# A mixture of experts behind an attention: the experts' rows in fixed slots of 512, what is left over by table

## The chip, the cores and the metric

The kernel runs on one core of a Trainium2 chip. Its five engines run side by side, each with its own queue of instructions that it works off in order: TensorE (PE in the profile, with its weight loads as PEld), VectorE (DVE), ScalarE (ACT), GpSimd (POOL) and SyncE (SP, which here only issues transfers). The metric is the device time of one execution in microseconds. Before the change it is 1090.66 us, the median of three runs (1090.1 to 1093.66).

## The reference

The input x is 4 batches of 1024 rows of 256. The first half is causal attention with 16 heads, whose projections go through a latent space, followed by a residual and a layer norm. The second half is a mixture of 8 experts with a Sinkhorn router:

```
scores = (x @ router_w.T + router_b) / temp
gates  = sinkhorn(scores)                     # 3 rounds over experts and over the rows of a batch
topk_vals, topk_idx = top_k(gates, 2)
topk_gates = topk_vals / sum(topk_vals)
expert e: (relu(x @ wg[e]) * (x @ wp[e])) @ wo[e]      # 256 -> 512 -> 256
x = layernorm(x + sum of the two picked experts, weighted by topk_gates)
```

Each row is wanted by two of the eight experts, so there are 8192 pairs of a row and an expert. The kernel computes only these pairs, not all 8 experts for each row. How many pairs an expert gets depends on the data.

## The kernel before

**The stages.** The attention runs batch by batch; the projections of the next batch and the output projection and routing of the one before are woven into it. Routing needs a whole batch, since Sinkhorn normalises over its rows. The pairs of batches 0 to 2 are therefore known during the attention of batch 3, and those of batch 3 only after it. The expert stage begins when the attention ends, with slots whose rows belong to the first three batches, while the last half batch is finished and routed beside them. At the end all rows are read back, normalised and written out.

**Lists and slots.** `pairs` is a table in device memory with a region for each expert. `route` works out for each pair its place in its expert's region and writes it there with indirect transfers on POOL (L808), 16 for each batch. `lay_out` turns the experts' counts into a table of slots, of 256 rows each: which expert, and where its rows begin. It is made twice: `lay_out(0)` for 17 slots that are surely full after three batches, `lay_out(1)` for the rest, up to 39 in all. SP reads expert and place from the table into registers (`value`, L896). 35 slots run always (`SURE`); if the data needs more, a branch runs the others (L1183).

**One slot.** `pairs_of` loads the list of 256 rows (L920), `weights` the expert's three weight matrices, 512 KB each (L943), `gather` the rows with two indirect transfers on POOL (L929). `rows` transposes the rows on TensorE (L973). All matrices are split into a high and a low part of fewer bits (`split`: ACT casts, L188, and DVE subtracts, L189), and a product is three matmuls (`mm3`, L195 to L197). `halves` does this for the weights, in 6 pieces of 512 columns. `slot` then makes, for each of four chunks f of the hidden size, the gate and the linear part in one PSUM bank of 512 columns, 256 for each (tile gp, from a ring of three banks); ACT takes the relu (L995), DVE multiplies (L996), and the result is split. After that come two output tiles (eo), which ACT scales (L1009) and POOL adds onto `results` in device memory with an indirect transfer (L1010). The adds of a slot wait for the landing of those of the slot before, since they may touch the same rows.

**Order.** `begin` is a generator: while slot n runs, it issues the transfers of later slots (`fetch`: lists 4 ahead, weights 2, gathers 3), transposes the rows of slot n + 1 and splits its weights. Weight tiles have two buffers as loaded and two as split, gathered rows three, eo six. A scheduler decides the final order of the instructions on each engine from priorities and its own estimate; on the engines that order is fixed. `in_turn` and `apart` only tell it which accesses may or may not pass one another.

Of the kernel before, what the change touches and what calls it, by code (L numbers as in the profile page):

```python
# [9 lines left out]
F32 = mybir.dt.float32  # L10
# [8 lines left out]
W_BUFS, GA, EA, EO = (2,3,4,6)  # L19
# [3 lines left out]
XG = 3  # L23
SCAT3 = 0.4
SH_A, SH_B, NSA = ((),(),0)
DZ = 3
SURE = 35
# [8 lines left out]
P = 128  # L36
# [7 lines left out]
def kernel(  # L44
# [35 lines left out]
    BT = B * T  # L80
    SR = 256
    RB = SR // P

    NA = -(-(2 * (B - 1) * T - E * (SR - 1)) // SR)
    NSLOT = (2 * BT + E * (SR - 1)) // SR
    REGION = BT + SR
    NLIST = (E - 1) * REGION + NSLOT * SR
# [12 lines left out]
    attn = actx.enter_context(tc.tile_pool(name="attn", bufs=1, side="right"))  # L100
    pctx = ctx.enter_context(ExitStack())
# [296 lines left out]
    def attend(unit):  # L398
# [25 lines left out]
        for g, qc in [(g, qc) for g in gs for qc in qcs]:  # L424
            q, k = stack(unit, g)
            for kb in range((qc + 1) * BPQ):
                lo = max(0, kb * P - qc * QC)
                n = f"{b}_{g}_{qc}_{kb}"
                pT = work.tile([P, HG, QC], F32, tag="pT", name=f"pT{n}", bufs=PT_BUFS)
# [33 lines left out]
    results = dram.tile([BT + SR, C], F32, name="results")  # L463
# [3 lines left out]
    base = const.tile([P, E], F32, name="base")  # L467
    for e in range(E):
        nc.gpsimd.memset(rank[:, e : e + 1], float(E - e))
        nc.gpsimd.memset(base[:, e : e + 1], float(e * REGION))  # L470
    ones = const.tile([P, P], F32, name="ones")
# [9 lines left out]
    slot_i = const.tile([1, NSLOT], I32, name="slot_i")  # L481
    nc.gpsimd.iota(slot_i, pattern=[[1, NSLOT]], base=0, channel_multiplier=0)
    slot_no = const.tile([1, NSLOT], F32, name="slot_no")
    nc.gpsimd.tensor_copy(slot_no, slot_i)

    def prepare():
# [5 lines left out]
        no_pair = work.tile([P, HG * QC], F32, tag="pT", name="no_pair", bufs=PT_BUFS)  # L492
        no_pair = no_pair[:, : 4 * PER].bitcast(I32).rearrange("p (n w) -> p n w", w=4)
        nc.gpsimd.iota(no_pair[:, :, 3], pattern=[[1, PER]], base=0, channel_multiplier=PER)
        nc.vector.tensor_single_scalar(no_pair[:, :, 0], no_pair[:, :, 3], SR - 1, ALU.bitwise_and)
# [5 lines left out]
            in_=mask[:, :C].unsqueeze(1).to_broadcast([P, RB, C]),  # L501
# [149 lines left out]
    def route(b):  # L651
# [141 lines left out]
        nc.vector.tensor_tensor(base, base, ps[:, NE : NE + E], ALU.add)  # L793
        at = sinkp.tile([P, 2, NB], F32, tag="so_a", name=f"so_a{b}")
# [26 lines left out]
    shift = tab("shift", [2, E])  # L821
    for e in range(E):
        nc.gpsimd.memset(shift[:, 0, e : e + 1], float(e * REGION))
        nc.gpsimd.memset(shift[:, 1, e : e + 1], float(e * REGION - SR + 1))
    zero = tab("zero", [E])
    nc.gpsimd.memset(zero, 0.0)
    used = zero
    tables = {}

    def lay_out(which):  # L830

        nonlocal used
        n_slots = NSLOT - NA if which else NA

        def t_(name, shape=(E,)):
            return tab(f"{name}{which}", shape)

        need = t_("need")
        nc.vector.tensor_tensor(need, base[:1], shift[:, which], ALU.subtract)
        needi = small.tile([1, E], I32, tag=f"needi{which}", name=f"needi{which}", bufs=1)  # L840
# [3 lines left out]
        nc.vector.tensor_tensor(need, need, used, ALU.subtract)  # L844
        yield 0.0
        upto = need
        for n in (1, 2, 4):
            nxt = t_(f"upto{n}")
            nc.vector.tensor_copy(nxt[:, :n], upto[:, :n])
            nc.vector.tensor_tensor(nxt[:, n:], upto[:, n:], upto[:, : E - n], ALU.add)  # L850
            upto = nxt
            yield 0.0
        hop = t_("hop")
        nc.vector.tensor_scalar(hop, need, -float(SR), float(REGION), ALU.mult, ALU.add)
        if which:
            more = t_("more")
            nc.vector.tensor_tensor(more[:, : E - 1], used[:, 1:], used[:, : E - 1], ALU.subtract)
            nc.vector.scalar_tensor_tensor(
                hop[:, : E - 1], more[:, : E - 1], float(SR), hop[:, : E - 1], ALU.mult, ALU.add
            )  # L860
        yield 0.0
        no = slot_no[:, :n_slots]
        past = t_("past", (n_slots, E - 1))
        nc.vector.tensor_tensor(
            past, no.unsqueeze(2).to_broadcast([1, n_slots, E - 1]),
            upto[:, : E - 1].unsqueeze(1).to_broadcast([1, n_slots, E - 1]), ALU.is_ge,
        )
        yield 0.0
        table = t_("table", (2, n_slots))
        nc.vector.tensor_reduce(table[:, 0], past, AX.X, ALU.add)  # L870
        nc.vector.tensor_tensor(
            past, past, hop[:, : E - 1].unsqueeze(1).to_broadcast([1, n_slots, E - 1]), ALU.mult
# [3 lines left out]
        nc.vector.scalar_tensor_tensor(table[:, 1], no, float(SR), table[:, 1], ALU.mult, ALU.add)  # L876
        if which:
            first = t_("first", (1,))
            nc.vector.tensor_scalar(first, used[:, :1], float(SR), None, ALU.mult)
            nc.vector.tensor_scalar(table[:, 1], table[:, 1], first, None, ALU.add)  # L880
        tablei = tables[which] = small.tile([1, 2, n_slots], I32, tag=f"ti{which}", name=f"ti{which}", bufs=1)
        nc.vector.tensor_copy(tablei, table)
        if which:
            tables["filled"] = small.tile([1, 1], I32, name="filled", bufs=1)
            nc.vector.tensor_copy(tables["filled"], upto[:, E - 1 :])
        if not which:

            used = t_("used")
            nc.vector.tensor_tensor(used, upto, need, ALU.subtract)
            nc.vector.tensor_scalar(used, used, -1.0, float(NA), ALU.mult, ALU.add)  # L890
            nc.vector.tensor_scalar_max(used, used, 0.0)
            nc.vector.tensor_tensor(used, used, need, ALU.min)
# [3 lines left out]
    def value(which, r, s, top):  # L896
        return nc.values_load(
            tables[which][0:1, r, s : s + 1], engines=[mybir.EngineType.SP], min_val=0, max_val=top,
            skip_runtime_bounds_check_because="worked out on the chip from counts that add up to 2 * B * T",
        )  # L900
# [10 lines left out]
    slots = {}  # L911

    def name_of(key):
        return f"{key[0]}_{key[1]}"

    def pairs_of(key):
        which, s = key
        row = value(which, 1, s, NLIST - SR)
        ent = const.tile([P, RB, 4], I32, name=f"ent_{name_of(key)}")
        ins = nc.sync.dma_start(out=ent, in_=pairs[bass.ds(row, SR)].rearrange("(p j) w -> p j w", j=RB))  # L920
        if not which:
            apart("pairs", "early", ins, ("last",))
        slots[key] = [ent, None, None, [], []]

    def gather(key):
        which = key[0]
        xg = slots[key][1] = early.tile([P, RB, C], F32, tag="xg", name=f"xg{name_of(key)}", bufs=XG)
        for j in range(RB):
            ins = nc.gpsimd.indirect_dma_start(  # L929
                out=xg[:, j], out_offset=None, in_=x1_rows[: BT if which else BT - T],  # L930
                in_offset=bass.IndirectOffsetOnAxis(ap=slots[key][0][:, j, 0:1], axis=0),
            )
            if not which:
                in_turn(ins)
                apart("x1", "early", ins, ("last",))

    def weights(key):
        which, s = key
        e = value(which, 0, s, E - 1)
        ws = slots[key][2] = []  # L940
        for i, (w, k, f) in enumerate(((wg_in, CC, FF), (wp_in, CC, FF), (wo_in, NFC, C))):
# [373 lines left out]
```

## Time and profile before

| | |
|---|---|
| time, median of three runs | 1090.66 us |
| the profiled execution, its own time | 1088.8 us |
| its span | 1087.1 us |
| busy TensorE / VectorE / ScalarE / GpSimd | 974.8 / 821.6 / 707.8 / 492.4 us |
| granted clock of TensorE over the span | 0.968 |
| moved by DMA | 146.33 MB |

The page gives busy time by engine, and the windows give the same for a stretch of the span. A busy TensorE is not TensorE at its peak: matmuls overlap, and the profile models their ends, so the distance from one start to the next tells the price of one. In a timeline a row has start, length, engine, line, operation and tiles; what stands in brackets is the idle time before it and what ended it. "SPq" is SP's queue of transfers.

### The profile page before, as it was taken

What the parts mean: (1) busy time and instruction counts of PE and PEld (TensorE: products, weight loads), DVE (VectorE), ACT (ScalarE), POOL (GpSimd) and SP (SyncE); (2) the same over time, 40 slices, a digit from 0 to 9 for tenths busy, and PEclk for the clock granted to TensorE, in tenths of its full rate; (3) what the DMA queues carried; (4) which work ended last, traced back from release to release, by engine and by line L of the source; (5) the groups of instructions that cost most, each with busy time, mean ns of one, the idle gap of its engine ahead of it and who ended that gap; (6) DMA issues with size and microseconds to landing.
All of it is one profiled execution on the core that took longest, in us unless ns stands there. A gap on an engine that the chain in (4) does not pass through costs nothing.

```text
span 1087.1 us, 20881 instructions
## 1 busy us (share of the span) xinstructions
PE 974.8 (90%) x6808; PEld 616.2 (57%) x6808; DVE 821.6 (76%) x2551; ACT 707.8 (65%) x1701; POOL 492.4 (45%) x552
## 2 busy tenths in 40 slices
PE   6689999999989999999899999999999699999940
PEld 4444333355434345533344333499999699999940
DVE  4768778888897888887538997398897588888716
ACT  3446666666776665676566776777776577877723
POOL 7167511121443624440423414645557756666545
PEclk9889999999999999999999999999999899999975
DMA  7663411231331312421123220587873788899638
GB/s 258 178 210 112 118 49 35 79 96 44 106 90 48 109 46 74 142 54 50 50 84 121 47 64 2 179 252 214 227 222 101 230 235 237 230 237 255 148 42 309
DMA packets 92065, 146.33 MB, mean 135 GB/s; under 512 B 19760, under 2 KB 55088, under 8 KB 91568
## 3 DMA queue, kind: packets, MB, share of 16 engines
q1 hardware_dynamic: 69296, 108.50, 31.6%
q0 software_dynamic: 20608, 36.18, 14.3%
q8 instruction: 56, 0.92, 0.3%
q10 hardware_dynamic: 2048, 0.27, 0.2%
q14 instruction: 57, 0.47, 0.1%
HBM read 109.26 MB, written 35.38 MB: 133 GB/s over the span
## 4 chain that ended last, share of the span: by engine, by line
PE 68%; DVE 8%; DMA 7%; ACT 6%; issue 4%; POOL 4%; SPq 2%; ACTq 0%; DVEq 0%; POOLq 0%
PE y L417 13%; PE s L354 10%; PE sT L433 9%; PE gp L195 5%; PE gp L196 5%; PE gp L197 5%; ACT pT L437 4%; POOL pairs L808 3%; PE eo L195 3%; PE eo L196 3%; PE eo L197 3%; PE po L591 2%; DVE mx L360 2%; DMA results<-eo,ent 2%; SPq L336 2%
## 5 line engine op out<-in xcount | busy, mean ns | idle before, releaser
L437 ACT ACTIVATE pT<-sT 128x512 f32<-128x512 f32 (+3 forms) x768 | 346.9, 491 | 178.4 <-PE sT L433 151.0
L363 DVE CUSTOM_DVE_ANT_0 d<-s,mask 128x128 bf16<-128x128 f32 (+3 forms) x512 | 237.0, 482 | 51.4 <-PE s L354 50.2
L433 PE MATMUL sT<-qs,ks 98*128 98x512 bf16 (+3 forms) x768 | 231.7, 328 | 16.4 <-ACT pT L437 11.6
L354 PE MATMUL s<-ks,qs 96*128 96x512 bf16 (+3 forms) x768 | 221.9, 331 | 22.5 <-DVE mx L363 7.8
L446 POOL TENSOR_SCALAR_AFFINE_SELECT pT<-pT 128x512 f32<-128x512 f32 x120 | 76.4, 637 | 273.1 <-ACT pT L437 256.8
L360 DVE TENSOR_REDUCE mx<-s 128x1 f32<-128x512 f32 x256 | 175.1, 684 | 29.4 <-PE s L354 28.3
L417 PE MATMUL y<-pT,va 128*32 128x512 f32 (+3 forms) x1536 | 181.9, 500 | 2.0 <-POOL pT L446 0.9
L1010 POOL DMA_INDIRECT results<-eo,ent x70 | 116.9, 1670 | 107.3 <-ACT hh L188 22.1
L189 DVE TENSOR_TENSOR wl<-w,wh 128x512 fp32r<-128x512 f32 x210 | 134.9, 685 | 37.7 <-ACT wh L188 37.4
L195 PE MATMUL gp<-xh,wh 128*128 128x256 f32 x560 | 159.5, 286 | 1.3 <-ACT xh L188 0.7
L197 PE MATMUL gp<-xh,wl 128*128 128x256 f32 x560 | 158.6, 284 | 0.5 <-DVE wl L189 0.5
L196 PE MATMUL gp<-xl,wh 128*128 128x256 f32 x560 | 158.9, 284 | 0.0
L354 PEld LDWEIGHTS <-qs 96*128 96x128 bf16 x768 | 71.6, 99 | 132.8 <-issue 101.0
L433 PEld LDWEIGHTS <-ks 98*128 98x128 bf16 x768 | 71.8, 98 | 122.9 <-issue 91.2
L188 ACT CAST wh<-w 128x512 fp32r<-128x512 f32 x210 | 117.6, 621 | 12.7 <-DMA w<-in_wg_dram 10.9
L195 PEld LDWEIGHTS gp<-xh,wh 128*128 128x128 f32 x560 | 106.0, 190 | 2.4 <-ACT xh L188 1.2
L197 PEld LDWEIGHTS gp<-xh,wl 128*128 128x128 f32 x560 | 106.3, 190 | 0.8 <-DVE wl L189 0.7
L196 PEld LDWEIGHTS gp<-xl,wh 128*128 128x128 f32 x560 | 106.3, 190 | 0.0
L929 POOL DMA_INDIRECT xg<-x_rows,ent x70 | 79.6, 1137 | 37.1 <-issue 17.4
L195 PE MATMUL eo<-wh,hh 128*128 128x256 f32 x280 | 80.1, 286 | 10.4 <-ACT hh L188 9.0
L808 POOL DMA_INDIRECT pairs<-ent,so_i x64 | 66.5, 1039 | 29.6 <-issue 18.4
L196 PE MATMUL eo<-wl,hh 128*128 128x256 f32 x280 | 79.1, 283 | 0.0
(207 smaller groups left out, 1603.1 us busy)
## 6 DMA issues: line engine op xcount, KB each, us to landing
w<-in_wg_dram SPq DMA_DIRECT2D x35, 512.0 KB, 6.2
w<-in_wp_dram SPq DMA_DIRECT2D x35, 512.0 KB, 5.6
w<-in_wo_dram SPq DMA_DIRECT2D x35, 512.0 KB, 4.7
ks<-parts SPq DMA_DIRECT2D x90, 128.0 KB, 2.8
qs<-parts SPq DMA_DIRECT2D x66, 128.0 KB, 2.9
parts<-lv POOLq DMA_DIRECT2D x12, 384.0 KB, 3.1
parts<-lv POOLq DMA_DIRECT2D x24, 192.0 KB, 3.1
xh<-in_x_t_dram SPq DMA_DIRECT2D x8, 512.0 KB, 5.8
```

The lines of the kernel that those rows point to most:

```text
L188: nc.scalar.copy(hi, src)
L189: (sub or nc.vector).tensor_tensor(lo, src, hi.bitcast(F32), ALU.subtract)
L195: nc.tensor.matmul(ps, lhsT=sh, rhs=mh, start=(i == 0), stop=False)
L196: nc.tensor.matmul(ps, lhsT=sh, rhs=ml, start=False, stop=False)
L197: nc.tensor.matmul(ps, lhsT=sl, rhs=mh, start=False, stop=(i == n - 1))
L354: nc.tensor.matmul(ps[:, :w], lhsT=q(h, half)[:NROW, t * P : (t + 1) * P], rhs=k(h, k0 // QC)[:NROW, :w], start=True, stop=True,)
L360: nc.vector.tensor_reduce(m, ps, AX.X, ALU.max)
L363: nc.vector.tensor_tensor_reduce(out=dump[:, :w], in0=ps[:, :w], in1=mask[:, QC - w :], scale=1.0, scalar=MASKED, op0=ALU.add, op1=ALU.max ...
L417: nc.tensor.matmul(acc[g, qc][SLOT * h : SLOT * (h + 1), lo:], lhsT=va[b % 2][:, kb, at : at + SLOT], rhs=pT[:, h, lo:], start=(kb == 0), ...
L433: nc.tensor.matmul(st[:, lo:], lhsT=k(h, kb // BPQ)[: NROW + 2, kb % BPQ * P : (kb % BPQ + 1) * P], rhs=q(h, qc)[: NROW + 2, lo:], start=T ...
L437: nc.scalar.activation(pT[:, h, lo:], st[:, lo:], AF.Exp, scale=scale)
L1010: ins = nc.gpsimd.indirect_dma_start(out=results[:, :], out_offset=bass.IndirectOffsetOnAxis(ap=ent[:, j, 1:2], axis=0), in_=eo, in_offset ...
```

## The change

The experts are no longer worked off by a table of slots of 256 rows. First come the rows 0 to 511 of each expert's region, experts 0 to 7, then the rows 512 to 1023, experts 7 to 0, and then what lies beyond row 1023, in slots of 256 rows by table. Of these three run always (`SURE = 3`), and up to 25 can be needed (`NOVER`). Expert and place of the first sixteen slots are known when the program is built, so they take no register, and the lists of all eight experts are loaded in one transfer for the first and one for the second 512. The expert that ends the first round begins the second, and its split weights are used again (`like`): so weights are split 15 times for the first sixteen slots and 3 times for the rest.

In slots of 512 rows gate and linear part have a PSUM bank each (tiles gp and lp), and the matmuls for them have 512 columns. hh and hl are now a tile for each chunk, six of each. Raw weights have one buffer instead of two, and each is loaded once the piece before it has been split; the gathered rows have two buffers of 512 rows instead of three of 256. After the third batch the counts are raised to at least 512 for each expert (`floor`), so that the last batch's pairs never fall into the first 512 rows, which are read early. `lay_out` is made once, for the rest alone. The tiles of the attention's exponentials move to a pool of their own (`exps`).

The core of the diff:

```
-W_BUFS, GA, EA, EO = (2,3,4,6)
+EO = 6
-XG = 3
+XG = 2
+HB = 6
-SURE = 35
+SURE = 3
...
+    ER = 512
     SR = 256
...
     REGION = BT + SR
-    NLIST = (E - 1) * REGION + NSLOT * SR
+    NOVER = (2 * BT - 4 * ER + 2 * (SR - 1)) // SR
+    NLIST = (E - 1) * REGION + 2 * ER + NOVER * SR
...
         nc.vector.tensor_tensor(base, base, ps[:, NE : NE + E], ALU.add)
+        if b == B - 2:
+            nc.vector.tensor_tensor(base, base, floor, ALU.max)
...
+    def pairs_of(k):
+        if k.which == 2:
+            row = value(1, k.s, NLIST - SR)
...
+        if k.which not in lists:
+            ent = lists[k.which] = const.tile([P, E, k.blocks, 4], I32, name=f"ents{k.which}")
+            regions = pairs[: E * REGION].rearrange("(e r) w -> e r w", r=REGION)
+            ins = nc.sync.dma_start(
+                out=ent.rearrange("p e j w -> p e (j w)"),
+                in_=regions[:, k.which * ER : (k.which + 1) * ER].rearrange("e (p j) w -> p e (j w)", p=P),
+            )
...
+    def weights(k, i):
+
+        if k.like is not None:
+            return
...
+        t = k.raw[i] = early.tile([P, n, f], F32, tag=f"w{i}", name=f"w{i}_{k.name}")
+        nc.sync.dma_start(out=t, in_=w[rows_e].rearrange("e (k p) f -> p (e k) f", p=P))
+
+    def halves(k, i):
+        if k.like is not None:
+            k.hl[i] = k.like.hl[i]
+            return
...
+            if 2 * R > QC:
+                gate, lin = (mx_tile(f"{i}p{k.name}_{f}") for i in "gl")
+            else:
+                both = mx_tile(f"gp{k.name}_{f}")
+                gate, lin = both[:, :R], both[:, R:]
+            for (h_, l_), ps in zip(k.hl, (gate, lin)):
+                mm3(ps, [(h_[:, c, cut], l_[:, c, cut], k.xh[:, c, :R], k.xl[:, c, :R]) for c in range(CC)])
+            r = early.tile([P, ER], F32, tag="relu", name=f"relu{k.name}_{f}", bufs=3)[:, :R]
+            nc.scalar.activation(r, gate, AF.Relu)
+            nc.vector.tensor_tensor(r, r, lin, ALU.mult)
...
+    first = [Slot(0, e) for e in range(E)]
+    second = [Slot(1, e) for e in reversed(range(E))]
+    second[0].like = first[-1]
+    further = [Slot(2, n) for n in range(NOVER)]
+
+    def begin_early():
+        pairs_of(first[0])
+        for i in range(3):
+            weights(first[0], i)
+        gather(first[0])
...
+    def begin(keys, n, given):
...
+        k, nxt = keys[n], keys[n + 1] if n + 1 < len(keys) else None
+        early_next = nxt is not None and (nxt.which == 0 or k.which > 0)
+        if n not in given and (k.which and (n == 0 or not keys[n - 1].which)):
+            pairs_of(k)
+            gather(k)
+        if early_next:
+            pairs_of(nxt)
+            gather(nxt)
...
+        for i in range(3):
+            halves(k, i)
+            if nxt is not None:
+                weights(nxt, i)
+            yield
...
+    run(first + second + further[:SURE], (0,))
...
+    with tc.If(filled > SURE):
+        added.clear()
+        with early_pool() as early, ffn_pool() as ffn:
+            run(further[SURE:])
```

## The prediction

> **What bounds the kernel now.** I read the page's busy shares first, then the windows by stage, then the timelines of the two places where TensorE stops.
>
> From part 1 of the page (engine, busy time, share of the span, instructions):
>
> ```profile
> PE 974.8 (90%) x6808; PEld 616.2 (57%) x6808; DVE 821.6 (76%) x2551; ACT 707.8 (65%) x1701; POOL 492.4 (45%) x552
> ```
>
> From the windows (stretch, then busy us and count of PE, PEld, DVE, ACT, POOL, then granted clock, DMA share, GB/s):
>
> ```profile
> 900.00:1000.00 100.00, 100.00 (x849) 100.00 (x848) 80.83 (x167) 79.83 (x191) 63.75 (x46) 1.00 0.88 236
> ...
> 1040.00:1087.00 47.00, 4.40 (x31) 3.63 (x29) 17.90 (x78) 11.77 (x24) 22.95 (x38) 0.58 0.62 196
> ```
> ```profile
> 840.00:850.00 10.00, 3.68 (x32) 3.47 (x30) 0.42 (x1) 0.39 (x1) 7.87 (x8) 0.81 0.33 73
> 850.00:860.00 10.00, 7.66 (x49) 7.66 (x50) 7.29 (x15) 7.71 (x17) 7.87 (x8) 0.68 1.03 321
> ```
>
> The attention ends and the expert stage begins at about 703.7 us; its last matmul ends near 1045.1. In that stage TensorE is never free except in one hole around 843 to 852, so the stage lasts as long as its matmuls. ACT and DVE are at 80% beside it and hidden. After 1045 TensorE is done and something else sets the end.
>
> How long a matmul takes is read from starts, because ends are modelled. Timeline of PE, first with 512 columns (the projection), then with 256 (an expert slot); start, modelled duration, engine, line:
>
> ```profile
> 17.54 0.40 PE L195 MATMUL qk_ps<-xT_h,wqk_h 128*128 128x512 f32 x1
> ...
> 19.81 0.39 PE L196 MATMUL qk_ps<-xT_l,wqk_h 128*128 128x512 f32 x1
> ```
> ```profile
> 912.27 0.28 PE L195 MATMUL gp<-xh,wh 128*128 128x256 f32 x1
> ...
> 914.05 0.28 PE L195 MATMUL eo<-wh,hh 128*128 128x256 f32 x1
> ```
>
> Ten steps in 2.27 us are 227 ns with 512 columns (230 over all undisturbed neighbours in the projection); fifteen in 1.78 are 118.7 ns with 256 (118.5 over all). That is nearly the same price per column, so the narrow matmul isn't far from streaming already.
>
> The hole, in SP's queue and on ACT:
>
> ```profile
> 826.25 0.37 SPq L943 DMA_DIRECT2D w<-in_wo_dram  x1
> 845.54 0.35 SPq L920 DMA_DIRECT2D ent<-pairs  x1
> 846.38 0.37 SPq L943 DMA_DIRECT2D w<-in_wg_dram  x1
> ```
> ```profile
> 851.37 0.62 ACT L188 CAST wh<-w 128x512 fp32r<-128x512 f32 x1 [10.94 <-DMA w<-in_wg_dram]
> ```
>
> The first list of the last batch (L920) waits for the sixteen scatters of POOL (L808, 820.1 to 844.4). The weights of that slot stand behind it in SP's queue, the cast behind the weights, hh behind the cast: TensorE stops from 843.5 to 852.3, 8.8 us. The low clock up to about 856 costs another 2 us.
>
> The end, on POOL:
>
> ```profile
> 1047.22 1.55 POOL L1010 DMA_INDIRECT results<-eo,ent  x1 [3.06 <-DMA results<-eo,ent]
> 1049.08 1.55 POOL L1010 DMA_INDIRECT results<-eo,ent  x1 [0.31 <-issue]
> 1053.63 1.55 POOL L1010 DMA_INDIRECT results<-eo,ent  x1 [3.01 <-DMA results<-eo,ent]
> ```
>
> Each slot's two adds wait until the adds of the slot before have landed: a link of 6.45 us. Links start at 1034.26, 1040.76, 1047.22 and 1053.63, and the first z load goes at 1060.79. So 15.7 us lie between the last matmul (1045.1) and the z loads.
>
> **The change part by part.** Sums are against the profiled execution: span 1087.1, its own time 1088.8. The median shown is 1090.66, 1.9 above it; the difference found is subtracted from the median.
>
> *Rows and matmuls.* Before: 35 slots of 256 rows, 8960 rows. After: 16 slots of 512 and 3 of 256, again 8960. The reference's routing of these inputs gives the experts 952, 937, 945, 1020, 1051, 995, 1219 and 1073 pairs; three exceed 1024, each by under 256, so three slots by table suffice and the branch for more isn't taken. Transposes (140) and eo matmuls (840 of 256 columns) stay. Of the gate and linear matmuls, 1536 narrow ones become 768 wide. By the rows above a wide one saves between 2 x 118.5 - 230 = 7 and 2 x 118.7 - 227 = 10.4 ns, 5 to 8 us; I take **-6.5**.
> [...]
>
> *Splits and weight loads.* Before, 35 weight sets are split, after 15 + 3 (the last expert's is used twice). 17 x 6 = 102 pieces fewer, each 621 ns on ACT (L188) and 685 on DVE (L189): 63 and 70 us of work, and 17 x 1.5 MB of loads. All of it lies under TensorE's busy time, so it is worth 0 by itself. It buys cover: for 512 rows ACT had 2 x (4 x 0.383 + 4 x 0.406 + 2 x 0.474 + 0.587 + 6 x 0.621) = 16.8 us of work against 18 of TensorE. After, with 512-column rows at about 0.60 (the attention's pT row), it has 8 x 0.60 + 4 x 0.474 + 2 x 0.59 + 6 x 0.62 = 11.6 against 17.5; DVE 16.2 before, 16 x 0.685 = 11.0 after. If the cover were gone, a late piece would cost its 0.6 to 0.7 us.
>
> *PSUM ring.* gate and linear now have a bank each in a ring of three. In plain order a bank is wanted again two groups, 2.7 us, after it was filled; relu (0.60) or multiply (0.69) frees it in under 1. But in the order in which the program issues, a slot's first three groups are opened together and closed one after another, and the fourth follows some 1.15 us after the first is closed. So 0 to 0.6 us a slot, times 16: 0 to 10; ACT's slack speaks for the low end: **+2**.
>
> *Start.* In SP's order the first slot's weights now stand among the stack loads of the last batch, where SP stood idle from 477.6 to 485.5: 0. The list for eight experts is one DMA instead of four (L920), but four gathers (L929, 1.28 us apart) must be through before the first transposes, 691.1 to 696.2 plus landing: before the attention's end at 702.5. The second weight set can only be loaded once the first is split (one raw buffer instead of two), which stalls ACT to about 719; TensorE meanwhile has 1.37 us per group plus the last batch's projections, about as much. The old start had some 4 us of short stalls: **0**, -3 to +3.
>
> *The middle.* so_ps, the last step of the routing on TensorE, stands 4 us of matmuls earlier; the scatters stand on POOL behind the first two adds of slot 4, so I expect them from about 815 to 839.5 (16 x 1.54 as before). Then POOL issues two adds (3.7), waits for the list, which lands near 844, and issues four gathers (5.1), landed near 851. The transposes stand behind 137.6 us of matmuls, when the issued order is added up at the prices above; with the 7 us of small stalls seen up to there before, about 848: 2.5 late. Worse, the adds of slot 5 stand behind the gathers, and free their eo buffers only near 854 (there are six, so the third tile of slot 6 takes that of the first of slot 5), while ACT wants it at 848; relu and casts stand behind that copy in ACT's queue, and the matmuls behind them. So a hole of about 6, plus 1 of low clock, replaces 8.8 + 2: **-3.8**, between -10.8 (none left) and +5. SP holds no late weights there: the doubled expert needs none.
>
> *The slots by table.* They have one raw buffer: 9 us of period against 5 to 6 of landing plus the split: **+1**, 0 to 4.
>
> *The end.* E is the end of the last matmul. In the issued order the last 512-row slot's eo groups end at E - 22 to E - 20.6, then the three small slots' at E - 13.7, E - 2.5 and E. The wide slot's four adds: from E - 23, 7.4 to issue and 3 to land, E - 12.7. Next link to E - 6.3. The next waits for its own eo, E - 3.3, and lands at E + 3.2; the last takes 7.15 to the z loads as in the rows: E + 10.4, where it was E + 15.7: **-5.3**.
>
> The registers (floor, one table instead of two) are a few DVE rows of 0.15 us under the attention: 0, behind sT and y on TensorE.
>
> Sum: -6.5 + 2 + 0 - 3.8 + 1 - 5.3 = **-12.6**: 1088.8 becomes 1076.2, and the median 1090.66 becomes **1078.0**.
>
> **The rivals.**
>
> *The hole closes.* If the eo buffers come free in time and the start is smooth: -6.5 - 5.3 - 10.8 + 1 = -21.6, 1069. For it: ACT and DVE have 35% slack, and the DMA queues, at 0.81 to 0.88 in this stage, lose half of the weights. Against: POOL's order above.
>
> *The hole stays as it was or grows by up to 5.* -12.6 + 3.8 to + 8.8: 1082 to 1087. For it: four gathers and four adds per wide slot stand in one in-order queue on POOL (12.5 of each 17.5 us), so anything late there stays late.
>
> *Slower: the three-bank ring.* If every wide group waits for its bank, 64 chunks pay. Break-even is 12.6 / 64 = 0.20 us a chunk; at 0.5 it is 32 us, less 12.6: 1110. [...] By the trace the old ring of three ran at 1.00 from 900 to 1000 without a pause. Against it: 2.7 us of distance against 0.9.
>
> *It doesn't do what it says.* A fourth slot by table would send all 22 remaining ones through the branch, 22 x 9 = some 200 us, 1280. Expert 3 has 1020 pairs, four from the limit.
>
> **How the numbers follow.** Forecast 47% (its own range 1073 to 1083); hole closes 22%; hole stays 15% (13 faster, 2 same); ring 15% (10 slower, 5 same); overflow 1%. Three in a thousand, 3.3 us, is about what can be told from no change. Faster 0.82, same 0.07, slower 0.11. The range 1064 to 1091 takes in the first three, with 5 us below the second, and the ring up to break-even; it leaves out about 15%.
>
> **What would show it.** Wide gp matmuls 227 to 230 ns apart and clock near 1.00; 108 weight pieces instead of 210; ACT and DVE well below 80%; one hole of about 6 us near 848, ended by ACT eo or xh; the first z load about 10 us after the last matmul. Wrong if waits on relu or multiply appear at each slot's start, if weights are late at the small slots, or if slots past the third run.

## The result and the profile after

The changed kernel takes 1075.91 us (median of four runs, 1073.72 to 1077.82) where the kernel before takes 1091.24 (four runs beside it): a ratio of 0.985, with a 95% interval from 0.982 to 0.988. The forecast was 1078.0. The profiled execution took 1073.72 us with a span of 1071.9, against 1088.8 and 1087.1 before: 15.2 us less of span, where the sum of the steps had said 12.6.

The engines over the span, from part 1 of the page of the changed kernel, and four stretches of it (busy us and count of PE, PEld, DVE, ACT, POOL, then granted clock, DMA share, GB/s):

```profile
PE 970.4 (91%) x6040; PEld 577.8 (54%) x6040; DVE 750.0 (70%) x2300; ACT 642.3 (60%) x1474; POOL 480.8 (45%) x551
```
```profile
840.00:850.00 10.00, 10.00 (x52) 8.30 (x51) 3.26 (x5) 3.73 (x7) 5.05 (x5) 1.00 0.83 219
850.00:860.00 10.00, 6.29 (x25) 5.08 (x25) 3.44 (x6) 4.09 (x8) 8.17 (x7) 0.67 0.57 80
900.00:1000.00 100.00, 99.28 (x581) 86.59 (x580) 55.30 (x88) 57.88 (x113) 56.14 (x43) 1.00 0.60 143
1030.00:1071.90 41.90, 5.74 (x46) 5.33 (x45) 18.84 (x81) 12.86 (x27) 19.54 (x36) 0.63 0.64 215
```

DVE and ACT lost 72 and 65 us of work and PE 4. ACT and DVE are at 55 to 58% in the steady stretch, where they were at 80, and PE isn't any freer for it. TensorE stops once, later than before (850 instead of 843) and for less long. Of what the change was to do, the trace has the 108 weight pieces (L189) where there were 210, and 144 narrow gp matmuls, which are three slots by table; the branch for more was not taken.

That stop, on PE, ACT, POOL and in SP's queue (start, duration, engine, line, operation, then the idle time before and what ended it):

```profile
850.96 0.95 PE L960 MATMUL xgT_ps<-ident,xg 128*128 128x128 f32 x3 [0.83 <-DMA xg<-x_rows,ents]
...
855.07 0.58 PE L196 MATMUL eo<-wh,hh 128*128 128x256 f32 x1 [2.56 <-ACT eo L994]
```
```profile
847.42 0.48 ACT L994 ACTIVATE eo<-eo,ents 128x256 f32<-128x256 f32 x1 [1.63 <-PE eo L198]
854.55 0.47 ACT L994 ACTIVATE eo<-eo,ents 128x256 f32<-128x256 f32 x1 [6.66 <-DMA results<-eo,ents]
```
```profile
845.60 1.01 POOL L921 DMA_INDIRECT xg<-x_rows,ents  x1 [3.77 <-DMA ents<-pairs]
...
849.44 0.94 POOL L921 DMA_INDIRECT xg<-x_rows,ents  x1 [0.30 <-issue]
850.69 1.62 POOL L995 DMA_INDIRECT results<-eo,ents  x1 [0.30 <-issue]
```
```profile
820.27 0.37 SPq L941 DMA_DIRECT2D w<-in_wo_dram  x1
841.24 0.37 SPq L910 DMA_DIRECT2D ents<-pairs  x1
```

Read from below: the second list (L910) leaves SP's queue only at 841.24, after the scatters (814.0 to 838.1). POOL waits for it till 845.60 and issues four gathers; the adds of slot 5 stand behind them, from 850.69. ACT waits 6.66 us, till one of them has landed and an eo buffer is free; PE's next eo group waits for ACT. The gathered rows come late as well, by 0.83 us and some more. In all PE loses 4.6 us there beyond the price of its matmuls (0.99 + 0.86 + 2.77 of neighbouring gaps), and the granted clock from 850 to 860 is 0.67.

The end, on POOL and in SP's queue:

```profile
1033.76 1.54 POOL L995 DMA_INDIRECT results<-eo,ent  x1 [2.54 <-ACT eo L994]
1038.72 1.54 POOL L995 DMA_INDIRECT results<-eo,ent  x1 [3.42 <-issue]
1040.57 1.54 POOL L995 DMA_INDIRECT results<-eo,ent  x1 [0.30 <-issue]
```
```profile
1045.98 3.75 SPq L1200 DMA_DIRECT2D z<-results  x8
```

The last matmul starts at 1036.02, the first z load at 1045.98: 10.0 us, where 15.7 lay before.

**An account of the 15.2 us.** From the starts on PE's timeline I priced each stretch (118.5 ns for a matmul of 256 columns, 229.7 for one of 512, which is the mean over its neighbours between 860 and 1000, 110 for transposes and the like) and took the price from its length. What is left is the excess: stops and low clock.

| part | before | after | difference |
|---|---|---|---|
| first gp matmul at | 703.7 | 704.4 | +0.7 |
| price of all of the stage's matmuls | 321.0 | 314.9 | -6.0 |
| excess, start to 742 | 4.9 | 3.3 | -1.5 |
| excess, 742 to 840 | 2.5 | 2.0 | -0.4 |
| excess, 840 to 862 | 10.8 | 7.1 | -3.7 |
| excess, steady stretch (862 to 1000; after: to 995) | 0.7 | 1.8 | +1.1 |
| excess, last slots | 1.7 | 2.5 | +0.8 |
| last matmul to first z load | 15.7 | 10.0 | -5.8 |
| z loads to the end | 26.3 | 25.9 | -0.4 |

The differences were taken before rounding. Of the -6.0, 768 x (2 x 118.5 - 229.7) = 5.6 is the wide matmul. The rest is four transposes of 0.11 that are only missing from the trace: both kernels issue 140, and 132 and 128 are recorded.

### The profile page after: what moved, and what is told of

It reads as the page before. It is cut to its first block, busy times and chain, and to the rows that moved or that the text cites. A ratio compares the mean times of both kernels' runs of the same rounds, so it can differ in the third digit from the quotient of the medians.

```text
span 1071.9 us, 18329 instructions
## 1 busy us (share of the span) xinstructions
PE 970.4 (91%) x6040; PEld 577.8 (54%) x6040; DVE 750.0 (70%) x2300; ACT 642.3 (60%) x1474; POOL 480.8 (45%) x551
## 3 DMA queue, kind: packets, MB, share of 16 engines
q0 software_dynamic: 20672, 36.41, 15.7%
## 4 chain that ended last, share of the span: by engine, by line
PE 66%; ACT 7%; DVE 7%; DMA 7%; issue 5%; POOL 5%; SPq 2%; ACTq 0%; POOLq 0%; DVEq 0%
PE y L418 13%; PE s L355 10%; PE sT L434 9%; ACT pT L438 4%; POOL pairs L813 3%; PE gp L197 3%; PE gp L198 3%; PE gp L196 3%; PE eo L196 2%; PE po L594 2%; PE eo L198 2%; PE eo L197 2%; DVE mx L361 2%; PE lp L197 2%; PE lp L198 2%
## 5 line engine op out<-in xcount | busy, mean ns | idle before, releaser
L995 POOL DMA_INDIRECT results<-eo,ents x64 | 105.2, 1643 | 73.6 <-ACT eo L994 57.3
L978 DVE TENSOR_TENSOR relu<-relu,lp 128x512 f32<-128x512 f32 x64 | 43.8, 684 | 62.4 <-ACT relu L977 46.7
L190 DVE TENSOR_TENSOR wl<-w,wh 128x512 fp32r<-128x512 f32 x108 | 70.0, 685 | 16.6 <-ACT wh L189 15.2
L813 POOL DMA_INDIRECT pairs<-ent,so_i x64 | 66.3, 1036 | 29.5 <-issue 17.8
L921 POOL DMA_INDIRECT xg<-x_rows,ents x64 | 64.5, 1008 | 31.7 <-issue 15.5
L977 ACT ACTIVATE relu<-gp 128x512 f32<-128x512 f32 (+1 forms) x76 | 42.7, 563 | 59.8 <-PE gp L198 59.1
L198 PE MATMUL eo<-wh,hl 128*128 128x256 f32 x280 | 78.1, 285 | 0.0
L418 PEld LDWEIGHTS y<-pT,va 128*32 128x32 f32 x1536 | 32.9, 108 | 76.6 <-issue 39.2
L190 DVE TENSOR_TENSOR hl<-relu,hh 128x512 fp32r<-128x512 f32 (+1 forms) x76 | 48.6, 648 | 26.6 <-ACT hh L189 25.9
L189 ACT CAST wh<-w 128x512 fp32r<-128x512 f32 x108 | 60.5, 619 | 9.5 <-PE gp L197 7.8
L197 PE MATMUL gp<-xl,wh 128*128 128x512 f32 (+1 forms) x176 | 65.2, 372 | 0.0
```

The costliest lines, as they stand in the source:

```text
L190: (sub or nc.vector).tensor_tensor(lo, src, hi.bitcast(F32), ALU.subtract)
L197: nc.tensor.matmul(ps, lhsT=sh, rhs=ml, start=False, stop=False)
L198: nc.tensor.matmul(ps, lhsT=sl, rhs=mh, start=False, stop=(i == n - 1))
L418: nc.tensor.matmul(acc[g, qc][SLOT * h : SLOT * (h + 1), lo:], lhsT=va[b % 2][:, kb, at : at + SLOT], rhs=pT[:, h, lo:], start=(kb == 0), ...
L813: ins = nc.gpsimd.indirect_dma_start(out=pairs[:, :], out_offset=bass.IndirectOffsetOnAxis(ap=ati[:, k, n : n + 1], axis=0), in_=ent[:, n, ...
L995: ins = nc.gpsimd.indirect_dma_start(out=results[:, :], out_offset=bass.IndirectOffsetOnAxis(ap=k.ent[:, j, 1:2], axis=0), in_=eo, in_offs ...
```

## The experiments

Three sets were run, of four kernels each, each with the kernel before beside it on the same chip. The chips of the first two sets take 1143 to 1145 us for the kernel before, that of the third 1093.6, so across sets only ratios to the kernel before are compared, and times only within a set. The kernel before has no trace on the chips of the first two sets.

### The change by itself on another chip

No edit; `a_same` is the changed kernel, run in the second set.

> The changed kernel, unaltered, so that the other kernels of this set can be held against it on one chip: 0.985 of the kernel before, the ratio measured first (0.982 to 0.988). If the chip alters what the change is worth, as the set before lets one suspect (the kernel before took 1144.6 us there), the ratio differs.

Measured: 1127.17 us against 1142.9, ratio 0.9858 (0.9835 to 0.9882). The change is worth the same on a chip that is 5% slower. Its trace is the yardstick for the kernels of the first two sets; those of the first set (`b_ea3`, `x_eo10`, `x_narrow`, `x_split2`) ran on another chip than it, one that takes 1144.6 us for the kernel before.

### What made the old hole: SP's order

`b_wfirst`, the kernel before, with weights ahead of the list:

```diff
-        for i, (step, depth) in enumerate(((pairs_of, EA), (weights, W_BUFS), (gather, GA))):
+        steps = [(0, pairs_of, EA), (1, weights, W_BUFS), (2, gather, GA)]
+        if n:
+            steps[:2] = steps[1::-1]
+        for i, step, depth in steps:
```

> The kernel before, with a slot's weights asked for ahead of the list in SP's queue instead of behind it; the list keeps its lead of four slots. Theory (SP, blocked by the list that waits for the scatters, made the hole at 843 to 852): the weights of that slot go at 826 as in any other, those of the next are held till 846 and are due at 852 or later: the hole and its low clock close, 8.8 to 10.8 us less, 0.990 to 0.992 of before. Rival (scatters or gathers set the hole, or instructions that come late): under 3 us, 0.997 or more. With the change worth 15 us in all, the rest of it, 4 to 6 us, would then be the end and the matmuls.

`b_ea3`, the same aim by one constant:

```diff
-W_BUFS, GA, EA, EO = (2,3,4,6)
+W_BUFS, GA, EA, EO = (2,3,3,6)
```

> The kernel before with one constant changed: the list of a slot is asked for three slots ahead instead of four, so it stands behind one more slot's weights in SP's queue. Theory (SP's blocked queue made the hole): the list waits for the scatters as before, till about 845.5, but only the weights of the slot after are now behind it, and these are due 9 us later: the hole at 843 to 852 closes, with its low clock, and the time falls by 8.8 to 10.8, to 1080 to 1083. Rival (the hole is set by something else in that stretch, the list, the gathers or the scatters themselves): another wait takes its place, less than 3 us are won, 1088 or more.

Measured: 1177.17 and 1172.49 us, ratios 1.0297 (1.0265 to 1.0329) and 1.0237 (1.0192 to 1.0281). Both are far slower, and neither theory nor rival had that. In the trace of `b_wfirst` the excess in the 31 us from 879 is 22 us. Its stops, on PE:

```profile
885.34 0.28 PE L197 MATMUL gp<-xh,wl 128*128 128x256 f32 x1 [0.79 <-issue]
...
886.76 0.28 PE L195 MATMUL gp<-xh,wh 128*128 128x256 f32 x1 [0.79 <-issue]
...
893.89 0.37 PE L195 MATMUL eo<-wh,hh 128*128 128x256 f32 x1 [1.51 <-issue]
895.30 0.37 PE L196 MATMUL eo<-wl,hh 128*128 128x256 f32 x1 [1.04 <-issue]
...
999.40 0.81 PE L976 MATMUL xgT_ps<-ident,xg 128*128 128x128 f32 x4 [2.22 <-DMA xg<-x_rows,ent]
```

Two things differ from what was meant. During the scatters (871.8 to 893.5) the matmuls come in groups of four, 1.4 us from group to group, and then singly; what they wait for the trace doesn't show ("issue"), but for 2.80 us at 890.2, for ACT's eo copy. And from 950 on the gathered rows are late slot after slot: 9.8 us of excess between 910 and 1050. The end is longer too: 20.2 us from the last matmul to the z loads, where the kernel before has 15.7. The edit moved more than SP's order: the instructions of POOL and PE stand in another order too. So these two kernels say nothing clean about the hole; for that the wait itself had to be shortened.

### What made the old hole: the wait for the scatters

`b_half` issues eight scatters instead of sixteen for the last batch, in the kernel before. It leaves out the second choice of that batch's rows, which then is missing from the output; the slots keep their size (146.32 MB moved, against 146.33). `b_same` is the kernel before unaltered:

```diff
-            for k in range(2):
+            for k in range(1 if b == B - 1 else 2):
                 ins = nc.gpsimd.indirect_dma_start(
                     out=pairs[:, :],
```

> The kernel before, with eight instead of sixteen scatters for the last batch: the second choice of its tokens isn't entered in the lists (their rows are left out of the output; all later work is of the same size). Eight scatters at 1.27 us pitch are 10 us of POOL. Theory (the list waits for the scatters, and the hole with it): the list goes 10 us earlier, the hole of 9 to 11 closes, 0.990 to 0.992 of before. Rival (the hole comes from elsewhere): less than 3 us, 0.997 or more. This undoes the wait without moving anything in SP's queue, which the two reordered kernels didn't: these cost 28 and 34 us.

> The kernel before, unaltered, for its trace on the same chip as the others of this set: ratio 1.000. Theory of the hole (SP's queue, blocked by the list that waits for the scatters): a stop of about 9 us near the end of the sixteen scatters, ended by a cast of late weights. Rival, from the traces of the two sets before (all engines stop during the scatters with nothing to wait for that the trace shows): 10 us or more of short stops while the scatters are issued, and the late weights are second to them.

Measured: `b_half` 1080.99 us, 0.9882 of before (0.9846 to 0.9919); `b_same` 1091.95, 0.9995 (0.9973 to 1.0016). SP's queue in `b_same` and then in `b_half`:

```profile
825.48 0.37 SPq L943 DMA_DIRECT2D w<-in_wo_dram  x1
844.77 0.35 SPq L920 DMA_DIRECT2D ent<-pairs  x1
845.62 0.37 SPq L943 DMA_DIRECT2D w<-in_wg_dram  x1
```
```profile
829.67 0.37 SPq L943 DMA_DIRECT2D w<-in_wo_dram  x1
838.51 0.35 SPq L920 DMA_DIRECT2D ent<-pairs  x1
839.36 0.37 SPq L943 DMA_DIRECT2D w<-in_wg_dram  x1
```

With half the scatters SP is held for 8.8 us instead of 19.3, the weights of that slot are in time, and the windows show what TensorE does with it:

```profile
820.00:862.00 42.00, 41.09 (x342) 40.34 (x341) 34.94 (x92) 32.43 (x78) 28.89 (x22) 1.00 0.71 198
```

No stop and a full clock. The excess there is 1.9 us (before, for 840 to 862 alone, 10.2 in `b_same`), and 11 to 12.6 us are won by the medians. In the traces the excess of the whole stage falls from 20.2 to 9.8; the two profiled executions are only 6.6 us apart, since the first gp of `b_half` comes 4.2 us later (707.1 against 702.9). So the hole hangs on the scatters, and its price, 8.8 + 2, is confirmed. Fewer scatters also let POOL's gathers and adds go earlier; that it was the list, the weights, the cast and hh that TensorE waited for rests on the rows of the traces.

### What makes the new hole

`a_half` is the same edit in the changed kernel, and leaves out the same pairs.

> The changed kernel, with the same eight scatters left out for the last batch. Theory (the new hole hangs on the scatters too: list, gathers and adds stand behind them on POOL): the hole, 7 us beyond the price of its matmuls in the first trace and 10 in the trace of the second set, goes: 5 to 9 us less than the changed kernel, 0.978 to 0.982 of before. Rival (the eo buffers alone make it): 0 to 3 us less. If both kernels lose the hole, what is left between them, 6 plus 5 us of matmuls and end, is what the change is worth without the middle: a_half over b_half about 0.99.

Measured: 1071.01 us, 0.9798 (0.9764 to 0.9831), 5 to 6 us below the changed kernel's 0.985 (0.982 to 0.988), and the intervals overlap a little. The traces decide: the excess from 820 to 862 is 0.2 us, where the changed kernel has 7.2. The new hole hangs on the scatters as well. `a_half` against `b_half` is 0.991: without any hole in either, about 10 us are left to the change, for matmuls and end.

`x_eo10` keeps all scatters and gives eo ten buffers:

```diff
-EO = 6
+EO = 10
```

> The changed kernel with ten buffers for eo instead of six, nothing else. Theory (the new hole near 850 is in its larger part the eo buffers that adds behind the gathers on POOL keep): the wait of 2.8 us on ACT's eo copy goes, with part of the low clock after it; the 1.9 us of waiting for the gathered rows stay: 1072 to 1073.5. Rival (eo is only the last in a chain that the gathers set): the wait moves to the next transposes or to POOL, less than 1 us is won, 1075 or more.

Measured in the first set: 1128.15 us, 0.9836 (0.9798 to 0.9875), no different from the changed kernel's 0.9858 on the other slow chip. By the trace it couldn't be: on these chips the hole isn't the one described above. PE in `a_same`, and what DVE shows at the same time:

```profile
880.50 0.79 PE L196 MATMUL gp<-xh,wh 128*128 128x512 f32 x1 [3.31 <-issue]
886.17 0.58 PE L196 MATMUL eo<-wh,hh 128*128 128x256 f32 x1 [2.98 <-issue]
```
```profile
880.48 0.69 DVE L190 TENSOR_TENSOR xl<-xgT_ps,xh 128x512 fp32r<-128x512 f32 x1 [4.09 <-issue]
```

There PE, DVE and ACT (idle for 6.45 us up to 879.86) stop together in the second half of the scatters, for nothing that the trace shows; the eo copies aren't late. The buffers' share had to be read on a chip without these stops, in `x_best`, below.

### The PSUM ring

`x_ring` puts the linear half into two idle banks in the second eight slots:

```diff
-                gate, lin = (mx_tile(f"{i}p{k.name}_{f}") for i in "gl")
+                gate = mx_tile(f"gp{k.name}_{f}")
+                lin = (bg_tile if k.which else mx_tile)(f"lp{k.name}_{f}")
```

> The changed kernel with the linear half of the second eight and of the small slots in two PSUM banks that stand idle by then, so that gate has the ring of three to itself. Theory (my +2 for the ring is about zero: the trace shows no wait on relu or multiply above 0.3 us in a slot): 0 to 1 us less than the changed kernel. Rival (the shared ring costs 0.2 us a chunk or more): 7 us less or more, over the second half of the stage.

Measured: 1119.92 us, 0.9799 (0.9777 to 0.9821), against 0.9858 of `a_same` in the same set: 7 us less by the medians, and the intervals don't meet. The traces can't show all of that: the profiled execution of `a_same` is the fastest of its six, and that of `x_ring` only 0.9 us faster. They show 2.1 us of excess in the steady stretch from 900 to 1040 that become 0.4, and the last matmul 7.9 us ahead of the z loads instead of 10.0, since the last slots' matmuls come in another order and one link of the chain of adds starts earlier; the last slots give 1.8 back (excess 4.4 against 2.6 from 1040 on). That is 2 us; the other 5 stay open. In the steady stretch of `a_same` no gate or linear group waits for its bank. What goes away is a wait of this kind, on PE:

```profile
959.54 0.66 PE L960 MATMUL xgT_ps<-ident,xg 128*128 128x128 f32 x4 [0.25 <-DVE xl L190]
```

The second transpose of every other slot waits for the split of the first (`xl`), 0.4 us from start to start beyond the price. The transposes have tiles of another pool (`st_tile`), so the two banks took this wait away by the order of the matmuls that came with them. That a bank was ever waited for in the changed kernel is not shown.

`x_best` has this ring and ten eo buffers, on the chip of the third set.

> The changed kernel with the linear half of the second eight in the two idle PSUM banks and ten eo buffers, the candidate for the fastest. Ring: 7 us by the medians of the set before, about 4 by its trace (2 in the steady stretch, 2 at the end). Ten eo buffers: nothing on chips where other stops set the hole (no difference from the changed kernel's ratio in the first set), 2.8 where they set it. So 0.978 to 0.982 of before; rival (the ring's gain was chance): 0.985.

Measured: 1071.86 us, 0.9796 (0.9760 to 0.9833), the fastest that gives the whole result: 2.0% below the kernel before, and 0.5% below the change alone by the ratios, whose intervals overlap. It is no better than the ring alone in the second set (0.9799), so by the medians nothing is left for the eo buffers; what they do is read from the trace. The steady stretch and the transition on PE:

```profile
870.00:990.00 120.00, 120.00 (x708) 105.60 (x707) 69.27 (x110) 70.35 (x137) 77.14 (x57) 1.00 0.66 143
```
```profile
856.97 1.39 PE L960 MATMUL xgT_ps<-ident,xg 128*128 128x128 f32 x4 [1.86 <-DMA xg<-x_rows,ents]
```

PE is busy for all of 120.00 us. In the hole the wait for ACT's eo copy has gone and only the wait for gathered rows remains: excess 4.3 where the changed kernel has 7.1. The ring has no part there yet, as it begins with the second eight slots. The 2.8 between them are as much as PE had waited for the eo copy (2.77); that is one execution of each, and no run has the ten buffers alone on such a chip.

### The wide matmuls

`x_narrow` issues each wide matmul as two of 256 columns into the same bank:

```diff
-                mm3(ps, [(h_[:, c, cut], l_[:, c, cut], k.xh[:, c, :R], k.xl[:, c, :R]) for c in range(CC)])
+                for q in range(0, R, SR):
+                    part = slice(q, q + SR)
+                    mm3(
+                        ps[:, part],
+                        [(h_[:, c, cut], l_[:, c, cut], k.xh[:, c, part], k.xl[:, c, part]) for c in range(CC)],
+                    )
```

> The changed kernel with each gate and linear matmul of the 512-row slots issued as two of 256 columns into the same bank; all else is as in the changed kernel. By the rows of before (118.5 against 227 to 230 ns): 768 times 7 to 10 ns, 5.4 to 8 us more, 1081 to 1084. By the rows of after in its steady stretch (229.7, against 2 x 118.0 there): 4.8 more, 1080.7. [...] Rival (the price is per column alone): no change, 1075.9.

Measured: 1142.87 us, 0.9985 (0.9963 to 1.0006), 1.3% or 14.5 us above the changed kernel's ratio: about twice what the price gives. In the steady stretch a slot takes 18.95 us instead of 17.88. Windows of the same stretch, `a_same` first:

```profile
950.00:1040.00 90.00, 89.27 (x530) 78.15 (x529) 50.89 (x81) 51.95 (x102) 48.51 (x36) 1.00 0.59 134
```
```profile
950.00:1040.00 90.00, 87.25 (x715) 85.65 (x714) 49.13 (x77) 49.49 (x96) 51.55 (x37) 1.00 0.58 135
```

PE idles 2.75 us of 90 instead of 0.73: once in every slot it waits 0.45 us for `xl`, as the narrow groups are in another order. The narrow matmuls are 120.0 ns apart in this kernel, not 118.5, so 48 pairs a slot cost 48 x (240.0 - 229.7) = 0.5 us more, which is 7.9 for all 768. The rest of the 1.07 a slot is this wait and smaller gaps that I didn't resolve. Beside that the transition is 9 us worse (excess 19.7 against 10.4), in the stops without a visible cause. So the wide form is worth the predicted 5 to 8 us by its price, and in this kernel about as much again by the order that comes with it.

### The splits

`x_split2` splits every weight piece twice:

```diff
-            split(*(t.rearrange("p k f -> p (k f)")[:, n * QC : (n + 1) * QC] for t in (hi, lo, w)))
+            for _ in range(2):
+                split(*(t.rearrange("p k f -> p (k f)")[:, n * QC : (n + 1) * QC] for t in (hi, lo, w)))
```

> The changed kernel with every weight piece split twice, 216 pieces on ACT and DVE instead of 108 (before: 210); loads and matmuls as in the changed kernel. Theory (splits are hidden under TensorE): 0 in the steady stretch; at the start, where ACT's first weights are late anyway, up to six pieces of 0.62 us more, so 1076 to 1079.5. Rival (fewer splits are where the gain came from): most of the 15 us are lost again, 1085 or more.

Measured: 1148.61 us, 1.0037 (1.0013 to 1.0061): with the number of splits of the kernel before all that the change wins is lost, 1.8% or 20 us. The theory falls for this kernel, and the rival has its number. POOL's rows (busy us, mean ns) in `a_same` and in `x_split2`:

```profile
L995 POOL DMA_INDIRECT results<-eo,ents x64 | 105.0, 1641 | 81.0 <-ACT eo L994 65.9 <-issue 7.6 <-DMA results<-eo,ents 3.1
...
L921 POOL DMA_INDIRECT xg<-x_rows,ents x64 | 64.5, 1008 | 40.7 <-PE xgT_ps L960 17.5 <-issue 16.7 <-DMA ents<-pairs 2.8
```
```profile
L996 POOL DMA_INDIRECT results<-eo,ents x64 | 125.5, 1960 | 68.5 <-ACT eo L995 33.3 <-ACT hh L189 8.8 <-ACT wh L189 7.9
L921 POOL DMA_INDIRECT xg<-x_rows,ents x64 | 79.1, 1235 | 41.2 <-PE xgT_ps L961 20.5 <-issue 17.3 <-DMA ents<-pairs 2.9
```

POOL didn't get a single instruction more and is busy 35 us longer with these two. The chip isn't the cause: the scatters of the same POOL (L813) take 1039 ns in `x_split2` and 1038 in `a_same`, and gathers and adds that meet no split take 988 and 1589 in `x_split2` too, as the table below has it. DVE and ACT both did more here, but the timeline of `x_split2` tells them apart. Sorted by what covers more than half of their first 0.9 us, a subtraction of a split on DVE (L190, wl or hl) or a cast of a split on ACT (L189, wh or hh), POOL's DMAs take, in mean ns (count):

| | neither | cast alone | subtraction alone | both |
|---|---|---|---|---|
| gather | 988 (34) | 1007 (7) | 1515 (8) | 1585 (21) |
| add | 1589 (23) | 1579 (11) | 1809 (9) | 2390 (27) |

So the longer issue goes with DVE's subtractions (1515 ns against 988, 1809 against 1589), and with a cast alone it isn't longer (1007 and 1579). The kernel before, sorted in the same way, has 1011 (28), 995 (4), 1369 (16) and 1153 (22) for its gathers and 1598 (28), 1592 (8), 1730 (7) and 1755 (27) for its adds, longer with a subtraction alone as well. Why it is so, no run shows. How much of the 20 us it costs stays open, for the program's order moved as well: the scatters start at 888 instead of 857, behind six more adds, and TensorE then waits long for its gathered rows:

```profile
921.57 0.69 PE L961 MATMUL xgT_ps<-ident,xg 128*128 128x128 f32 x2 [18.56 <-DMA xg<-x_rows,ents]
```

Against `a_same` the excess is 13.9 us more in the transition, 3.1 in the steady stretch, 3.5 ahead of the transition and 4.3 at the small slots, and the first gp comes 5.8 us later.

### The order of the last slots

`x_last512` puts the small slots ahead of the last 512-row slot:

```diff
-    run(first + second + further[:SURE], (0,))
+    run(first + second[:-1] + further[:SURE] + second[-1:], (0,))
```

> The changed kernel with the three slots by table ahead of the last 512-row slot instead of behind it. Theory (the end is a chain of slots whose adds wait for those of the slot before, and then the pace of POOL): in the issued order the last small slot's eo ends 9.7 us before the last matmul, its adds land about 2.5 before it; the four adds of the last slot follow at 1.85 each and land 3 later, about 7.5 after the last matmul, where it was 9.8: 2 us less than the changed kernel. Rival (the end is bound by the last eo and its landing alone, about 5 us): 5 less. Rival (four adds at the end instead of two make the chain longer): up to 3 more.

Measured: 1124.28 us, 0.9813 (0.9785 to 0.9841) against 0.9858 of `a_same`: the medians are 2.9 us apart, but the intervals overlap, so that it is faster is likely and not shown. In the trace the end is 8.4 us long instead of 10.0, near the 7.5 of the theory and not the 5 of the first rival; but the stage has 3.4 us more of excess, from waits on ACT's xh in the small slots (up to 1.2 us). The chain of adds is what sets the end; another order shifts the loss elsewhere.

## Why the prediction was right

Taken by its own steps, against the account above:

- **Rows and matmuls, -6.5.** The price difference came to 7.3 ns for each wide matmul, 5.6 us, at the low end of the stated 5 to 8. Splitting the matmuls again costs at least that. The wide ones are 229.7 ns apart between 860 and 1000, with PE busy for 99.28 of the last 100 us of it.
- **Splits and weight loads, 0.** In the steady stretch before, PE was at 100.00 of 100 us with ACT and DVE at 80%, so nothing was to be won there at once, and the account has nothing for it. But "worth 0 by itself" was argued from ACT's and DVE's slack alone. `x_split2` shows a second path, DVE's work to POOL's issue times (gathers 1235 ns instead of 1008, adds 1960 instead of 1641) to the scatters and adds, and a third, the order in which the program then issues. On the first chip POOL's gathers went from 1137 to 1008 ns and its adds from 1670 to 1643 with the change: 64 x 0.13 + 64 x 0.03 = 10 us of POOL less; where that was on the path, the account can't tell. Of this step the words "0 by itself" failed. Given back to the changed kernel, the splits cost 20 us, with the order that came of it, while the kernel before carried as many with 3.2 us of excess from 742 to 840 and 862 to 1000 together. So the fewer splits won nothing where they were, but the wide slots as built need them. The prediction had said that they buy cover, but had worked it out from the time of ACT and DVE alone; that its 0 held is in part luck.
- **PSUM ring, +2.** The excess of the steady stretch grew by 1.1, and with two more banks it goes. The size was about right, the mechanism wrong: the wait is at the transposes, and no fourth group waits for a bank. That is luck.
- **Start, 0.** +0.7 for the later first matmul and -1.5 of excess after it. The first slot's four gathers were through in time, as predicted (its transposes begin at 697.83). What came late is the fourth gather of the second slot, issued at 699.61 behind two stores; its transpose stands ahead of the first gp in PE's order, and the granted clock from 705 to 710, when the first wide matmuls came, was 0.85:

```profile
703.45 0.47 PE L960 MATMUL xgT_ps<-ident,xg 128*128 128x128 f32 x1 [2.43 <-DMA xg<-x_rows,ents]
```

- **The middle, -3.8.** -3.7 by the account. The mechanism came as described, line by line: adds behind gathers on POOL, eo buffers free near 854, ACT's copy and then PE late. I had said a hole of 6 plus 1 of clock; it is 4.6 of gaps plus 2.5 of low clock and smaller waits. `a_half` shows that the scatters stand behind it; that the eo buffers hold 2.8 of it is what the traces of `x_best` and of the changed kernel suggest.
- **Slots by table, +1.** +0.8.
- **The end, -5.3.** -5.8. The adds of the last link went at 1038.72, 2.7 us after the start of the last matmul, where the working had 3.2 after its end.

The steps sum to -12.6 and the account to -15.2; the 2.6 between them are the end and the z loads (0.9), the ring (0.9), the start (0.8), the stretch from 742 to 840 (0.4) and smaller parts, less 0.5 for the price of the matmuls, which was put too high. No step missed by more than a microsecond. The forecast held as each stretch was costed at the wait that ends last in it, and the largest fall of work, 63 and 70 us of splits on ACT and DVE, was put at nothing.

Of the rivals, the closing hole is what the two half kernels then brought about by other means, and `x_best` in part; the slower ring is excluded by the steady stretch, at 99.28 of 100 us; the fourth slot by table did not come.

## What to carry to other kernels

Price each stretch of the bounding engine from its starts and look at the excess; a change that takes 70 us from each of two engines beside a third moved the end by 15 us, of which 6 are the price of its matmuls and most of the rest lies at two places (a hole and a tail) that the shares of the span don't show. A wait in an in-order queue is tested by making what it waits for shorter: moving instructions in the program lets a scheduler move others too, and two such tests here cost 28 and 34 us without telling anything of the wait. In `x_split2` twice the splits, on ACT and DVE beside TensorE, went with longer issues on the engine that issues the indirect transfers (POOL's gathers 1235 ns instead of 1008); before putting hidden work at nothing, look at that engine's mean durations too.

## What the runs showed of the hardware

Four things that I had not expected. First, the same kernel takes 5% longer on some chips: 1143 to 1145 us against 1091 to 1094, with equal durations of single instructions (POOL's adds 1641 ns in `a_same` and 1643 in the changed kernel's first trace, its gathers 1008 and its 512-column selections 637 in both), and with stops of PE, DVE and ACT together (in `a_same` 3.31, 4.09 and 6.45 us, up to 880.5; PE's longest 5.20, in `x_last512` at 888.16), in which no instruction shown is waited for. Most of the loss, some 43 us, lies ahead of the expert stage (first gp of `x_ring`, which is the changed kernel up to its second eight slots, at 747.9; of the changed kernel in its first trace at 704.4). What causes these stops stays open, and so does whether the two reordered kernels would have lost as much on a chip without them. Second, the mean issue time of POOL's gathers and adds rose by a fifth when DVE and ACT had twice the splits to do (1008 to 1235 ns, 1641 to 1960; the scatters stayed at 1038 and 1039), and a gather that met a subtraction alone took half as long again (1515 ns against 988). Third, the narrow gate matmuls of `x_narrow` ran at 120.0 ns apart, those of the kernel before at 118.2 and those of `b_wfirst`, on a slow chip as well, at 118.3, with the same tiles and the same modelled length of 0.28 us; I can't say why. Fourth, 512 columns cost 229.7 ns and 256 cost 118.5; by an estimate from these two, with all the rest growing with the columns, 2 x 118.5 - 229.7 = 7.3 ns of each matmul are fixed.
